# A copy of each scatter's row numbers on GpSimd, in an attention-and-experts block

## The chip, the cores and the metric

The kernel runs as one program on one core of a Trainium2 chip. The metric is the device time of one execution in microseconds (us), taken as the median of three runs. The engines named below are PE (TensorE, matrix products and transposes), DVE (VectorE), ACT (ScalarE), POOL (GpSimd) and SP (SyncE, which here only issues DMAs). Each engine takes its own instructions in the order in which they stand in the program.

## What is computed

The input `x` holds 4 sequences of 512 tokens with 128 features. A first half, a gated convolution block, replaces the attention. A second half is a mixture of 160 experts, of which each token takes 8. The heart of the second half, cut to what matters here (`x` is the normalized and modulated input of that half):

```python
probs = sigmoid(x @ router_w.T + expert_bias)
top_w, top_idx = top_k(probs, 8)
top_w = 2.5 * top_w / (sum(top_w) + 1e-9)
h1 = silu(einsum('th,eih->eti', x, w_gate))          # 160 experts, 64 inner columns
routed = einsum('eti,ehi->th', h1 * combine.T[:, :, None], w_down)   # combine: top_w at top_idx
out = routed + silu(x @ w_gate_shared.T) @ w_down_shared.T
x = x + gb * out
```

## The kernel before

The four sequences are handled one after the other by a generator, `sequence(b)`. Its pieces are interleaved by hand, so that the second half of one sequence runs beside the first half of the next. One sequence has 512 tokens, which lie on 128 partitions in 4 groups (`NT = 4`).

The experts don't compute every token. Each token is written 8 times into a table in device memory, once per chosen expert, at a row that belongs to that expert. There are two tables: `tables[0]` for sequences 0 and 1 and `tables[1]` for sequences 2 and 3, each with 17,408 rows of 128 numbers. Then `experts(s)` reads table `s` in 34 / 2 = 17 blocks of 1,024 rows (`xg`, a plain load issued by SP on L611), transposes each on PE (`px`, L616), multiplies by the experts' weights (`ph` on L639 and L675, `py` on L649 and L685), and stores the products in the same row order in `results[s]` (L629). Last, `combine(b)` fetches the 8 result rows of each token (`yk`, L725), weighs and adds them.

What happens around the change, in `sequence(b)`:

- DVE computes in `keys` (the 8 largest keys of a token), `ikey` (L491) and `slot_in` (L493) the table row of every token and choice: `slot_in` has 128 partitions, 4 groups and 8 choices, 32 row numbers per partition. The normalized tokens lie in `h2` (L433).
- Then come 4 x 8 = 32 scatters (L498). Each is one indirect DMA that POOL issues. It takes one column of `slot_in`, 128 row numbers, and writes 128 rows of 512 bytes from `h2[:, t, :]` to those rows of the table. The 32 scatters of a sequence are called a burst below. They are declared free of dependencies on each other. In four sequences there are 128 scatters.
- DVE later reads `slot_in` again (`row`, L544) to make the row numbers for the fetches.

POOL's other work: five small powers (L242) in the first 55 us, the 128 scatters, then in `combine` 128 indirect fetches (L725) and, for sequences 0 and 1 alone, a product of each fetched block with its weight (L702). In `combine` of those two sequences, the order fetch, product, fetch, product is written out by hand with `behind(b, "weight")` and `behind(b, "fetch")`. `behind(b, what)` lets instructions stand in their engine's order after the instruction that was noted in `last[what, b]`; it makes no wait.

`experts(0)` needs both bursts of table 0 to have landed, and is laid among the instructions of sequences 2 and 3. `experts(1)` needs the bursts of sequences 2 and 3. The fetches of sequences 0 and 1 need all of `results[0]`, and those of sequences 2 and 3 all of `results[1]`. POOL takes its instructions in order, so the fetches also come after all scatters.

Buffers: `own(b, shape, dtype, tag, name)` gives one buffer per tag and parity of `b`, so sequence `b + 2` takes over the buffers of sequence `b` and waits for their last readers. `keys` and, after the change, `pick` have the tag `"keys"`, so they share one buffer.

The order of instructions on each engine, where it isn't fixed by `behind`, is planned when the program is built, from estimated durations (`schedule_with_timeline_sim=True` in `kernel`). The planner also draws the semaphore waits. Adding instructions can thus shift the order of others.

Of the kernel before, what the change touches and what calls it, by code (L numbers as in the profile page):

```python
# [34 lines left out]
U32 = mybir.dt.uint32  # L35
# [5 lines left out]
P = 128  # L41
# [4 lines left out]
E, INTER, TOPK = 160, 64, 8  # L46
# [10 lines left out]
NT = L // P  # L57
# [35 lines left out]
def adaln_block(  # L93
    ctx: ExitStack, tc: tile.TileContext, x_rows, vecs, wmod, mats, lines, w_gd, w_dsT, w_ov, out_rows
):
    nc = tc.nc
# [19 lines left out]
    def own(b, shape, dtype, tag, name):  # L116
        return work.tile(shape, dtype, tag=f"{tag}{b % 2}", name=f"{name}_{b}", bufs=1)
# [24 lines left out]
    tables, results = [], []  # L142
    for i in range(2):
        t = dram.tile([ROWS, D], F32, tag=f"table{i}", name=f"table{i}")
        tables.append(t)
        t = dram.tile([ROWS, D], F32, tag=f"result{i}", name=f"result{i}")
# [32 lines left out]
    for eps in (1e-5, 1e-6):  # L179
# [7 lines left out]
        out=tri, in_=ones16, compare_op=ALU.is_gt, fill=0.0, base=0, pattern=[[1, P]], channel_multiplier=-1  # L187
# [88 lines left out]
    ready, halves, keep, last = {}, {}, {}, {}  # L276

    def behind(b, what):
        return tc.issue_after(last[what, b].ins) if (what, b) in last else nullcontext()
# [4 lines left out]
    def sequence(b):  # L284
# [61 lines left out]
        for k in range(DC):  # L346

            at, to, n = ds(32 * k, 32), max(0, 1 - k), L - abs(k - 1)
# [56 lines left out]
        for half in range(2):  # L405
            pl = bank(b, f"pl{b}_{half}")
            for i in range(2):
                t = 2 * half + i
# [13 lines left out]
        for half in range(2):  # L422
            for t in (2 * half, 2 * half + 1):
# [3 lines left out]
                    out=repl[:, t, :], in_to_replace=top[:, t, :], in_values=prob[:, t, :], imm_value=-1.0  # L427
                )
            at = ds(2 * half, 2)
# [33 lines left out]
        keys = own(b, [P, NT, TOPK], F32, "keys", "keys")  # L463
        k2 = ranks[:, 0:4, :].rearrange("p (h i) e -> p h i e", h=2)
        for half in range(2):
            pr = spare(ps_y, "y", f"pr{b}_{half}")
            for i in range(2):
                t = 2 * half + i
# [23 lines left out]
        slot_in = own(b, [P, NT, TOPK], U32, "slot_in", "slot_in")  # L492
        last["slots", b] = nc.vector.tensor_single_scalar(slot_in, ikey.bitcast(U32), 0x7FFF, ALU.bitwise_and)  # L493


        for t in range(NT):
            for k in range(TOPK):
                ins = nc.gpsimd.indirect_dma_start(  # L498
                    out=tables[b // 2], out_offset=bass.IndirectOffsetOnAxis(ap=slot_in[:, t, k : k + 1], axis=0),
                    in_=h2[:, t, :], in_offset=None, bounds_check=ROWS - 1, oob_is_err=False,  # L500
                ).ins
                tc.declare_no_dep(ins, group=f"dispatch{b // 2}", reason="different rows")
                tc.add_to_no_dep_group(f"dispatch{b // 2}", ins)

# [287 lines left out]


    parts = [sequence(b) for b in range(B)]
    w_pairs = [weights(g) for g in range(NGO - 2)]
    next(parts[0])
# [100 lines left out]
    with tc.If(flags[0] + flags[1] > 0):  # L897
# [7 lines left out]
        for part in range(3):  # L905
            for odd in range(2):
                at = sel4[:, :, odd, :, :]
                nc.gpsimd.affine_select(
                    out=at, in_=at, compare_op=ALU.not_equal, fill=1.0, base=-part * ECH - 3 * odd,
# [56 lines left out]
```

## Time and profile before

| What | Value |
|---|---|
| median of 3 runs | 467.53 us (467.45 to 467.7) |
| the profiled execution | 600.99 us |
| its span, first to last instruction | 599.3 us |
| POOL busy | 286.5 us of the span |
| DVE busy | 222.8 us |
| ACT busy | 149.7 us |
| scatters (L498) | 128, 128.6 us busy in all |
| fetches (L725) | 128, 125.0 us busy in all |

The profiled execution took 133 us longer than the median of the runs that weren't profiled. That gap is far larger than the difference between runs, so durations from the trace can't be added up to the median without asking which of them belong to both.

A row of the timeline gives the start and the duration in us, engine, line, operation, the written and the read tiles, the count, and in brackets the idle time before it with what ended it. A row of the table of waits gives the waiting engine, line and tile, then what it waited for, the total in us, the number of times and the longest. "Issue" means that the profile shows nothing that was waited for. "Remote", or "another core or an unknown queue", means that the wait's end has no event in the profile that could have ended it; on a program of one core it can't be another core.

The four bursts, from the timeline of POOL:

| Burst | first scatter starts | last scatter ends | length |
|---|---|---|---|
| sequence 0 | 71.29 | 113.83 | 42.5 us |
| sequence 1 | 136.73 | 178.30 | 41.6 us |
| sequence 2 | 212.86 | 254.35 | 41.5 us |
| sequence 3 | 292.39 | 333.19 | 40.8 us |

### The profile page before, as it was taken

What the parts mean: (1) busy time and instruction counts of PE and PEld (TensorE: products, weight loads), DVE (VectorE), ACT (ScalarE), POOL (GpSimd) and SP (SyncE); (2) the same over time, 40 slices, a digit from 0 to 9 for tenths busy, and PEclk for the clock granted to TensorE, in tenths of its full rate; (3) what the DMA queues carried; (4) which work ended last, traced back from release to release, by engine and by line L of the source; (5) the groups of instructions that cost most, each with busy time, mean ns of one, the idle gap of its engine ahead of it and who ended that gap; (6) DMA issues with size and microseconds to landing.
All of it is one profiled execution on the core that took longest, in us unless ns stands there. A gap on an engine that the chain in (4) does not pass through costs nothing.

```text
span 599.3 us, 7468 instructions
## 1 busy us (share of the span) xinstructions
PE 300.1 (50%) x2540; PEld 199.1 (33%) x2540; DVE 222.8 (37%) x747; ACT 149.7 (25%) x290; POOL 286.5 (48%) x334
## 2 busy tenths in 40 slices
PE   5998880399205973169721487847376640000000
PEld 3645440154102432147511365726265530000000
DVE  7637860288106490037700343201113202233332
ACT  2545331334105400044200121415155630000000
POOL 1001277406760067700377100088888707887773
PEclk9999795569755977568955587878599965555555
DMA  8999951003224021134841288956489941121211
GB/s 293 409 393 392 420 201 49 35 0 107 88 79 154 8 104 52 49 134 157 279 145 52 100 281 273 327 189 220 136 276 335 310 161 42 45 61 57 71 53 45
DMA packets 50366, 98.55 MB, mean 164 GB/s; under 512 B 7633, under 2 KB 26130, under 8 KB 48914
## 3 DMA queue, kind: packets, MB, share of 16 engines
q1 hardware_dynamic: 35856, 60.61, 28.9%
q10 hardware_dynamic: 6274, 20.62, 9.1%
q0 software_dynamic: 8192, 16.79, 8.9%
q8 instruction: 22, 0.36, 0.2%
q14 instruction: 22, 0.18, 0.1%
HBM read 50.54 MB, written 47.45 MB: 164 GB/s over the span
## 4 chain that ended last, share of the span: by engine, by line
PE 36%; another core or an unknown queue 20%; DMA 11%; issue 11%; POOL 10%; DVE 7%; ACT 3%; SPq 1%; ACTq 0%; DVEq 0%; POOLq 0%
POOL yk L725 9%; DMA xg<-table 7%; PE pc L356 5%; PE px L616 4%; PE py L649 3%; PE ph L321 3%; PE ph L675 3%; PE py L373 2%; PE ph L639 2%; DMA result<-yg 1%; PE pl L413 1%; DMA mat<-in_mats 1%; PE pu L345 1%; PE py L685 1%
## 5 line engine op out<-in xcount | busy, mean ns | idle before, releaser
L498 POOL DMA_INDIRECT table<-h,slot_in x128 | 128.6, 1005 | 151.5 <-DVE slot_in L493 60.9
L725 POOL DMA_INDIRECT yk<-result,row x128 | 125.0, 977 | 105.2 <-ACT yg L628 56.2
L616 PE MATMUL px<-ident,xg 128*128 128x128 f32 x272 | 49.8, 318 | 28.5 <-DMA xg<-table 16.9
L649 PE MATMUL py<-w_g,h 64*64 64x128 f32 x640 | 31.5, 329 | 50.8 <-ACT h L644 28.0
L616 PEld LDWEIGHTS px<-ident,xg 128*128 128x128 f32 x272 | 34.8, 160 | 39.4 <-issue 29.7
L649 PEld LDWEIGHTS py<-w_g,h 64*64 64x64 f32 x640 | 23.9, 163 | 57.2 <-ACT h L644 30.2
L709 DVE SCALAR_TENSOR_TENSOR out_sb<-yk,wk,out_sb 128x128 f32<-128x128 f32 x56 | 20.0, 356 | 52.3 <-DMA yk<-result,row 52.1
L639 PE MATMUL ph<-xs,w_g 128*64 128x64 f32 x640 | 32.8, 247 | 8.0 <-issue 7.3
L627 ACT COPY yg<-py 128x512 f32<-128x512 f32 x34 | 19.9, 585 | 67.7 <-PE py L649 41.0
L711 DVE TENSOR_TENSOR out_sb<-out_sb,yk 128x128 f32<-128x128 f32 x48 | 14.8, 314 | 57.6 <-POOL yk L702 43.6
L617 DVE COPY xs<-px 128x512 f32<-128x512 f32 x34 | 22.6, 684 | 35.7 <-remote 19.5
L356 PE MATMUL pc<-val,dia 128*128 128x512 f32 x72 | 32.0, 595 | 0.0
L639 PEld LDWEIGHTS ph<-xs,w_g 128*64 128x64 f32 x640 | 26.8, 155 | 13.9 <-issue 11.1
L386 DVE TENSOR_TENSOR x<-po,h 128x512 f32<-128x512 f32 x4 | 2.8, 692 | 76.7 <-remote 76.1
L303 PE MATMUL px_h<-ident,hn 128*128 128x128 f32 x16 | 3.9, 374 | 54.2 <-ACT hn L302 32.1
L644 ACT ACTIVATE h<-ph 128x512 f32<-128x512 f32 x20 | 11.9, 597 | 66.8 <-remote 57.7
L702 POOL TENSOR_TENSOR yk<-yk,wk 128x128 f32<-128x128 f32 x64 | 26.1, 414 | 1.0
L361 DVE SCALAR_TENSOR_TENSOR s<-val,vec,s 128x512 f32<-128x512 f32 x32 | 24.0, 750 | 0.7
L685 PE MATMUL py<-ow,h 64*128 64x128 f32 x224 | 16.8, 291 | 11.4 <-ACT h L680 8.4
L321 PE MATMUL ph<-hf,in_wn 128*128 128x512 f32 x32 | 20.6, 785 | 1.7 <-ACT hf L305 1.7
L617 ACT COPY xs<-px 128x512 f32<-128x512 f32 x34 | 18.9, 589 | 9.8 <-PE px L616 5.7
L303 PEld LDWEIGHTS px_h<-ident,hn 128*128 128x128 f32 x16 | 2.5, 161 | 55.9 <-ACT hn L302 32.7
(230 smaller groups left out, 528.7 us busy)
## 6 DMA issues: line engine op xcount, KB each, us to landing
table<-early SPq DMA_DIRECT2D x2, 8704.0 KB
xg<-table SPq DMA_DIRECT2D x34, 512.0 KB
result<-yg ACTq DMA_DIRECT2D x34, 512.0 KB
ow<-in_w_ov SPq DMA_DIRECT2D x112, 96.0 KB
w_g<-in_w_gd SPq DMA_DIRECT2D x10, 1024.0 KB
table<-h,slot_in POOLq DMA_INDIRECT x128
yk<-result,row POOLq DMA_INDIRECT x128
prob_kept<-prob ACTq DMA_DIRECT2D x4, 320.0 KB
```

Source lines behind the costliest of these rows:

```text
L321: nc.tensor.matmul(ph, in_wn[:, ts(o, P)], hf, start=True, stop=True)
L356: nc.tensor.matmul(pc, dia[:, k, :], val[:, 0, k : k + L], start=(k == 0), stop=(k == KS - 1))
L361: last["conv", b] = nc.vector.scalar_tensor_tensor(s[:, 1, :], val[:, 1, k : k + L], v("sym_k", KS + k), s[:, 1, :], ALU.mult, ALU.add)
L498: ins = nc.gpsimd.indirect_dma_start(out=tables[b // 2], out_offset=bass.IndirectOffsetOnAxis(ap=slot_in[:, t, k : k + 1], axis=0), in_=h2 ...
L616: nc.tensor.transpose(px[:, c, :], xg[:, 4 * half + c, :], ident)
L617: (nc.scalar.copy if s else nc.vector.tensor_copy)(xs[:, ds(4 * half, 4), :], px)
L639: nc.tensor.matmul(ph[ds((r ^ (j & 1)) * INTER, INTER), j, :], w[:, j, 0, ds(r * INTER, INTER)], xs[:, :, ds(16 * j + 8 * r, 8)], start=Tr ...
L649: nc.tensor.matmul(py[j & 1][ds(r * BLK, BLK), j // 2, :], h[at, j, :], w[at, j, 1, :], start=True, stop=True)
L685: nc.tensor.matmul(py[r][:, c, :], h[at, c, :], ow[at, c, r, ds(r * INTER, D)], start=True, stop=True)
L702: last["weight", b] = nc.gpsimd.tensor_mul(row, row, wk[:, t, k : k + 1].to_broadcast([P, D]))
L709: nc.vector.scalar_tensor_tensor(acc, yk[:, k, :], wk[:, t, k : k + 1], acc, ALU.mult, ALU.add)
L725: last["fetch", b] = nc.gpsimd.indirect_dma_start(out=yk[:, k, :], out_offset=None, in_=results[b // 2], in_offset=bass.IndirectOffsetOnAx ...
```

## The change

Each scatter no longer takes its row numbers from `slot_in`. POOL first copies the 128x1 column to a tile `pick` of the same shape (32-bit unsigned), and the scatter takes them from there. `behind(b, "scatter")` puts each copy after the scatter before it in POOL's order. Since the scatter reads what the copy wrote, it waits for that copy. The bounds check, the rows written and the table are the same.

```diff
+        pick = own(b, [P, NT, TOPK], U32, "keys", "pick")
         for t in range(NT):
             for k in range(TOPK):
-                ins = nc.gpsimd.indirect_dma_start(
-                    out=tables[b // 2], out_offset=bass.IndirectOffsetOnAxis(ap=slot_in[:, t, k : k + 1], axis=0),
+
+                at = pick[:, t, k : k + 1]
+                with behind(b, "scatter"):
+                    last["pick", b] = nc.gpsimd.tensor_copy(at, slot_in[:, t, k : k + 1])
+                last["scatter", b] = nc.gpsimd.indirect_dma_start(
+                    out=tables[b // 2], out_offset=bass.IndirectOffsetOnAxis(ap=at, axis=0),
                     in_=h2[:, t, :], in_offset=None, bounds_check=ROWS - 1, oob_is_err=False,
-                ).ins
+                )
+                ins = last["scatter", b].ins
                 tc.declare_no_dep(ins, group=f"dispatch{b // 2}", reason="different rows")
                 tc.add_to_no_dep_group(f"dispatch{b // 2}", ins)
```

## The prediction

> **What bounds the kernel now.** I read the chain of waits in order of time first, then the table of waits, then POOL's timeline, then PE's where the experts begin. The chain's longest pieces:
>
> ```profile
> 91.30 17.72 another core or an unknown queue
> 114.38 3.26 another core or an unknown queue
> 156.69 25.70 another core or an unknown queue
> 225.75 32.65 another core or an unknown queue
> 299.27 22.83 another core or an unknown queue
> 322.71 14.83 another core or an unknown queue
> ```
>
> Each row is a start, a length and what held the chain. All six lie inside a burst of scatters or just behind it, and end at the latest 4.4 us after the burst does (258.40 against 254.35, 337.54 against 333.19). Together they are 117.0 us. The table of waits names who stood there:
>
> ```profile
> DVE x L386 <- remote: 76.1, 3, 32.6
> ACT h L644 <- remote: 57.7, 4, 25.3
> POOL table L498 <- DVE slot_in L493: 60.9, 2, 38.0
> POOL yk L725 <- DMA result<-yg: 18.7, 1, 18.7
> ```
>
> DVE and ACT wait for nothing that the profile can show, L386 takes only `po` and `h`, and PE had done `po` by then. POOL meanwhile goes on at an even pace. So the other engines stand still while POOL scatters, for no reason of data.
>
> Do the unprofiled runs have this standstill? Take the 117.0 us out. The fetches, which start at 389.43, would start at 272.4. The POOL chain from there is 87.6 us of fetches and products (389.43 to 477.0), then the 18.7 us wait for the last results, then 103.5 us (495.76 to 599.3). PE has two unexplained waits of 6.24 and 6.56 us at 399 and 427 in that part, and in 389 to 440 does 340 matmuls against 553 in the 50 us after; without that the 18.7 us wait should nearly vanish. 272.4 + 87.6 + 103.5 is 463.5, plus 1.7 around the span (600.99 - 599.3) is 465.2. The median is 467.5. So I read the standstill as belonging to the profiled execution alone, and all but 2.3 us of the timed runs as explained without it. In them the bound is: the sequences and `experts(0)`, up to 272, then POOL with its fetches to the end.
>
> POOL's pace, first in a burst, then in a fetch with a product between:
>
> ```profile
> 174.78 0.97 POOL L498 DMA_INDIRECT table<-h,slot_in  x1 [0.30 <-issue]
> 176.06 0.97 POOL L498 DMA_INDIRECT table<-h,slot_in  x1 [0.30 <-issue]
> ...
> 508.98 0.41 POOL L702 TENSOR_TENSOR yk<-yk,wk 128x128 f32<-128x128 f32 x1
> 509.55 1.02 POOL L725 DMA_INDIRECT yk<-result,row  x1 [0.16 <-issue]
> 510.58 0.42 POOL L702 TENSOR_TENSOR yk<-yk,wk 128x128 f32<-128x128 f32 x1
> 511.16 1.02 POOL L725 DMA_INDIRECT yk<-result,row  x1 [0.16 <-issue]
> ...
> 587.12 0.94 POOL L725 DMA_INDIRECT yk<-result,row  x1 [0.30 <-issue]
> 588.37 0.94 POOL L725 DMA_INDIRECT yk<-result,row  x1 [0.30 <-issue]
> ```
>
> From start to start a scatter takes 1.275 us, a bare fetch 1.25, a fetch with a product 1.61. The product adds 0.36, though it lasts 0.41: it fills part of the 0.30 us that lies empty between two bare DMAs.
>
> **What the Trainium skill says.** Perfetto Trace Analysis, section "GPSIMD Engine Instruction": a GpSimd span in a profile is unreliable, and one should go by start-to-start spacing. The rows agree (0.97 shown, 1.275 paced), so I price by spacing. The same page, "DMA Instruction — SWDGE (GPSIMD)": the shown end is that of descriptor generation, not of the data. The trace agrees: the last fetch ends at 590.55, and DVE uses it at 592.25, 1.7 us later. GPSIMD Engine Reference, section "2.1 Instruction dispatch": every Pool instruction is broadcast and dispatched by software, some tens of cycles, so a 128x1 copy is nearly all overhead. The 128x1 IOTA at 1.27 us with 0.13 fits. SBUF — State Buffer, section "Who interferes with whom": a DVE instruction with two SBUF inputs contends with a GpSimd instruction that reads SBUF. The copies read SBUF; no row of this trace shows the effect.
>
> **The change, part by part.** Removed: nothing but the scatter's direct reading of `slot_in`. Added: 128 copies on POOL, and in each scatter a wait for its copy. Moved: nothing by hand; the planned order can shift.
>
> *A copy.* No row shows a 128x1 copy on POOL. The 128x1 memsets at the start last 0.10, the IOTA 0.13, the 128x128 product 0.41. I take 0.13.
>
> *The wait.* No row shows POOL waiting for its own result. A scatter that waited for `slot_in` in burst 3 started 0.28 us after it (292.11 to 292.39); in bursts 1 and 2, 0.27 and 0.28. That is my figure. Lower end: 0.16, the gap after a product. Upper end: 0.45, if the wait makes POOL's sequencer hold the scatter back undecoded; the first scatters of bursts 0 to 2 last 1.57, 1.59 and 1.38 in place of 0.97, so a cold start can cost that much and more.
>
> *The cycle.* Scatter 0.97, plus 0.04 as fetches after a product are longer by that at least (0.98 to 1.02 against 0.94), 0.03 to the copy, copy 0.13, wait 0.28: 1.45 us, 0.175 more than now. Lower end: 0.97 + 0.03 + 0.10 + 0.16 = 1.26, a little under today's 1.275. Upper end: 1.02 + 0.03 + 0.25 + 0.45 = 1.75; the middle of the upper part, 1.6, I price below.
>
> *Where it lies.* In time without standstill, `slot_in` is ready for the four bursts at 71.3, 115.75 (136.73 less 21.0), 166.2 (212.86 less 46.7) and 213.1 (292.39 less 79.3), and a burst lasts 40.8 to 42.5. POOL idles 2 to 9 us between bursts. With 32 x 0.175 = 5.6 us more, burst 0 ends at 119.4, burst 1 starts then and ends at 166.6 (157.3 before), burst 2 at 213.7, burst 3 at 260.2. The fetches start at 272.4, so POOL's own queue keeps 12 us of slack. Behind a waiting scatter stand only the next copies and scatters of POOL.
>
> *Who waits for the burst.* `experts(0)`. Its first load needs bursts 0 and 1 landed (1.7 us) and takes about 4.0 (the chain has an `xg` load of 4.04): ready at 163.0 before, 172.3 after. PE reaches it here:
>
> ```profile
> 215.70 1.11 PE L616 MATMUL px<-ident,xg 128*128 128x128 f32 x4 [1.64 <-DVE key L516]
> 217.75 1.11 PE L616 MATMUL px<-ident,xg 128*128 128x128 f32 x4 [0.94 <-DVE xs L617]
> 219.07 5.22 PE L373 MATMUL py<-s,w_sym 128*128 128x512 f32 x8 [0.20 <-ACT s L364]
> ```
>
> 215.70 less 46.7 is 169.0. There were 6.0 us of cover; after, the load is 3.3 us late. PE is in order, and behind these transposes stands L373 of sequence 3, on the chain. So up to 3.3 us reach the path. Some is absorbed: PE idles 1.64 and 0.94 us there anyway, and a planner that sees longer bursts would put the transposes later. I take 2.0 us. Burst 3 and `experts(1)` have 12 us of cover; the fetches and everything after 272 are untouched.
>
> *DVE against the copies.* At most 32 x 0.13 = 4.2 us per burst if every copy met a two-input DVE instruction; DVE is busy 14.1 of 20 us at the start of burst 0, and only a part of that with such instructions. I take one us, beside PE's work: nothing on the path. The shared `keys` buffer makes sequence b + 2 wait for burst b, over long before: nothing.
>
> Sum: 467.5 + 2.0 = 469.5 us, made on the standstill-free account of the profiled execution and laid onto the median.
>
> **Rivals.**
> A, the forecast: a cycle of about 1.45, 469.5 us (467.8 to 472).
> B, hidden: the cycle stays under 1.37, as the copy fills the empty 0.30 us; burst 1 ends within the 6.0 us of cover; 467.5. For it: the product costs less than it lasts. Against it: the product waits for no copy.
> C, POOL becomes the bound: a cycle of 1.6. Burst 1 ends at 71.3 + 84.1 + 64 x 0.325 = 176.2, the load is ready at 181.9, 12.9 us late: 480.4. The fetches would be 6.9 us late, inside that. From 1.545 on, POOL's queue alone reaches 272.4.
> D, the other side: the timed runs do have some of the standstill, and a Pool instruction between two scatters relieves it, as PE stands less in the fetches with products. It decides as soon as the relief exceeds A's 2 us. With my account only 2.3 us are left unexplained, which gives 465.2 with copies hidden. If fetches in timed runs are faster than in the profile, the unexplained part and the gain are larger, 10 us or more. A luckier planned order falls here too, by a few us.
> That the copies do not stand between the scatters is excluded, as the scatter reads the copy.
>
> **How the numbers follow.** A measurement of this kernel tells a change from none at about 0.2%, 0.93 us. Chances: A 0.42 (0.36 beyond 468.5, 0.06 inside), B 0.18 (0.16 inside, 0.02 under), C 0.13, D 0.27, of which 0.08 under 462. So faster 0.29, same 0.22, slower 0.49. The range from 462 to 480 leaves out the far part of D and half of C. The likeliest case alone: 467.8 to 472.
>
> **What would show it.** Copies of about 0.13 us in POOL's timeline, scatters 1.4 to 1.5 us apart, bursts of 45 to 48 us. In the profiled execution the standstill may shrink a great deal, so its span may fall by tens of us while the median hardly moves; that would confirm the account above. A median that falls by more than 1% would refute it: then the standstill is in the timed runs too. Scatters 1.6 us apart or more mean C.

## The result, and the profile after

| | kernel before | kernel after |
|---|---|---|
| median | 467.49 us (4 runs, 464.45 to 467.7) | 482.46 us (4 runs, 481.26 to 483.67) |
| profiled execution | 600.99 us, span 599.3 | 481.98 us, span 480.3 |

The change makes the kernel 3.4% slower: the ratio is 1.0336, with an interval of 1.03 to 1.0371. That is 15 us where 2 were forecast, and just above the range of 462 to 480. The profiled execution of after takes as long as its unprofiled runs. Lines below L498 stand six lines further down in the new kernel: the copy is L502, the scatter L503, the transposes of the experts L622, the fetches L731, the products L708.

The page of after, engines first, then the costliest groups (busy us, mean ns of one, idle time before them and what ended most of it):

```profile
PE 276.9 (58%) x2540; PEld 185.6 (39%) x2540; DVE 223.9 (47%) x747; ACT 149.4 (31%) x290; POOL 321.0 (67%) x462
...
L503 POOL DMA_INDIRECT table<-h,pick x128 | 132.7, 1037 | 37.9 <-POOL pick L502 35.9
...
L622 PE MATMUL px<-ident,xg 128*128 128x128 f32 x272 | 46.3, 311 | 52.1 <-DMA xg<-table 49.5
...
L502 POOL COPY pick<-slot_in 128x1 uint32<-128x1 uint32 x128 | 30.1, 235 | 22.8 <-DVE slot_in L493 22.2
```

POOL has 34.5 us more work (321.0 against 286.5): the copies' 30.1 and 4.1 more in the scatters. Beside that stand 35.9 us in which scatters wait for their copies. None of it says yet what reaches the end. For that, look at the third group: the experts' transposes wait 49.5 us for the loads of their blocks. PE's timeline shows where:

```profile
158.06 1.16 PE L589 MATMUL psh<-wds,hs 64*128 64x128 f32 x8 [0.68 <-ACT hs L586]
179.57 1.09 PE L622 MATMUL px<-ident,xg 128*128 128x128 f32 x4 [20.36 <-DMA xg<-table]
181.45 1.12 PE L622 MATMUL px<-ident,xg 128*128 128x128 f32 x4 [0.78 <-DVE xs L623]
182.77 3.78 PE L373 MATMUL py<-s,w_sym 128*128 128x512 f32 x4 [0.20 <-ACT s L364]
```

A single wait of 20.36 us, and L373 of sequence 3, which has nothing to do with that block, stands behind it. POOL's timeline gives the pace. First beside DVE, at the head of burst 0; then undisturbed, at the end of burst 1; last the first fetch:

```profile
72.70 0.68 POOL L502 COPY pick<-slot_in 128x1 uint32<-128x1 uint32 x1
73.66 1.43 POOL L503 DMA_INDIRECT table<-h,pick  x1 [0.28 <-POOL pick L502]
75.10 0.75 POOL L502 COPY pick<-slot_in 128x1 uint32<-128x1 uint32 x1
...
172.41 0.98 POOL L503 DMA_INDIRECT table<-h,pick  x1 [0.28 <-POOL pick L502]
173.40 0.19 POOL L502 COPY pick<-slot_in 128x1 uint32<-128x1 uint32 x1
173.87 0.98 POOL L503 DMA_INDIRECT table<-h,pick  x1 [0.28 <-POOL pick L502]
...
289.86 1.00 POOL L731 DMA_INDIRECT yk<-result,row  x1 [13.57 <-DMA xg<-table]
```

The undisturbed cycle is 0.98 + 0.19 + 0.28 = 1.45 us, as predicted. The disturbed one is 2.46 (a scatter of 1.43, a copy of 0.75, the wait of 0.28). DVE's timeline at that moment:

```profile
72.59 0.75 DVE L361 SCALAR_TENSOR_TENSOR s<-val,vec,s 128x512 f32<-128x512 f32 x1
73.26 0.32 DVE L522 TENSOR_TENSOR key<-key,pn 128x160 f32<-128x160 f32 x1
73.49 2.33 DVE L361 SCALAR_TENSOR_TENSOR s<-val,vec,s 128x512 f32<-128x512 f32 x3
75.74 0.17 DVE L550 TENSOR_SCALAR row<-slot_in 128x32 uint32<-128x32 uint32 x1
```

Both long copies end just after an instruction of L361 does (73.38 beside 73.34, 75.85 beside 75.82). L361 reads two tiles of 512 columns and a column of scalars (`vec`) from SBUF. The section "Who interferes with whom" of the Trainium skill's page SBUF — State Buffer says that a DVE instruction with two SBUF inputs contends with a GpSimd instruction that reads SBUF, and that their shared ports are an exclusive lock. The trace agrees in the main: these copies take 0.68 and 0.75 us where an undisturbed one takes 0.19, and all 15 copies of the trace that last over 0.3 us end 0.02 to 0.06 us after a DVE instruction does; of the other 113, 18 do. But not every overlap costs: copies at 70.58 and 115.54, which started just after an instruction of L361, took 0.18 and 0.19.

### The profile page after: what moved, and what is told of

Its sections match the earlier page's. It is cut to its first block, busy times and chain, and to the rows that moved or that the text cites. A ratio compares the mean times of both kernels' runs of the same rounds, so it can differ in the third digit from the quotient of the medians.

```text
span 480.3 us, 7716 instructions
## 1 busy us (share of the span) xinstructions
PE 276.9 (58%) x2540; PEld 185.6 (39%) x2540; DVE 223.9 (47%) x747; ACT 149.4 (31%) x290; POOL 321.0 (67%) x462
## 5 line engine op out<-in xcount | busy, mean ns | idle before, releaser
L503 POOL DMA_INDIRECT table<-h,pick x128 | 132.7, 1037 | 37.9 <-POOL pick L502 35.9
L731 POOL DMA_INDIRECT yk<-result,row x128 | 125.3, 979 | 44.0 <-issue 28.8
L622 PE MATMUL px<-ident,xg 128*128 128x128 f32 x272 | 46.3, 311 | 52.1 <-DMA xg<-table 49.5
L622 PEld LDWEIGHTS px<-ident,xg 128*128 128x128 f32 x272 | 33.9, 158 | 60.5 <-issue 42.9
L502 POOL COPY pick<-slot_in 128x1 uint32<-128x1 uint32 x128 | 30.1, 235 | 22.8 <-DVE slot_in L493 22.2
L645 PE MATMUL ph<-xs,w_g 128*64 128x64 f32 x640 | 27.8, 240 | 0.0
L655 PE MATMUL py<-w_g,h 64*64 64x128 f32 x640 | 24.7, 297 | 4.6 <-ACT h L650 4.5
L708 POOL TENSOR_TENSOR yk<-yk,wk 128x128 f32<-128x128 f32 x64 | 26.2, 414 | 1.1
L645 PEld LDWEIGHTS ph<-xs,w_g 128*64 128x64 f32 x640 | 23.9, 150 | 4.7 <-issue 2.6
L361 DVE SCALAR_TENSOR_TENSOR s<-val,vec,s 128x512 f32<-128x512 f32 x32 | 24.0, 751 | 0.7
L655 PEld LDWEIGHTS py<-w_g,h 64*64 64x64 f32 x640 | 19.2, 144 | 8.6 <-ACT h L650 5.9
L356 PEld LDWEIGHTS pc<-val,dia 128*128 128x128 f32 x72 | 13.4, 189 | 16.7 <-issue 16.7
L691 PEld LDWEIGHTS py<-ow,h 64*128 64x128 f32 x224 | 13.6, 187 | 13.3 <-ACT h L686 12.8
```

The source lines that it names most:

```text
L356: nc.tensor.matmul(pc, dia[:, k, :], val[:, 0, k : k + L], start=(k == 0), stop=(k == KS - 1))
L361: last["conv", b] = nc.vector.scalar_tensor_tensor(s[:, 1, :], val[:, 1, k : k + L], v("sym_k", KS + k), s[:, 1, :], ALU.mult, ALU.add)
L502: last["pick", b] = nc.gpsimd.tensor_copy(at, slot_in[:, t, k : k + 1])
L503: last["scatter", b] = nc.gpsimd.indirect_dma_start(out=tables[b // 2], out_offset=bass.IndirectOffsetOnAxis(ap=at, axis=0), in_=h2[:, t, ...
L622: nc.tensor.transpose(px[:, c, :], xg[:, 4 * half + c, :], ident)
L645: nc.tensor.matmul(ph[ds((r ^ (j & 1)) * INTER, INTER), j, :], w[:, j, 0, ds(r * INTER, INTER)], xs[:, :, ds(16 * j + 8 * r, 8)], start=Tr ...
```

## The experiments

The theory after the result: the loss comes through one place. Burst 1 ends late, the first load of `experts(0)` is late by as much, and PE, which takes its instructions in order, passes on the whole delay to sequence 3. The rival: the loss comes from all bursts, or from POOL's own queue up to the fetches.

### Copies in one pair of sequences alone

```diff
-        pick = own(b, [P, NT, TOPK], U32, "keys", "pick")
+        pick = own(b, [P, NT, TOPK], U32, "keys", "pick") if b < 2 else None
...
+                at = pick[:, t, k : k + 1] if b < 2 else slot_in[:, t, k : k + 1]
+                if b < 2:
```

The second run has `b >= 2` in the same three places.

> Copies in bursts 0 and 1 alone. Theory 'late first block': the whole loss comes from the end of burst 1, which holds back the first load of table 0 and with it PE; so the time stays at 481 to 484 us, and PE waits some 20 us for its first xg, as in the changed kernel. Rival 'POOL's queue': the loss is the sum of all slower bursts, so half of the copies cost about half, 474 to 476. In the profiled execution the standstill of the other engines should be gone in bursts 0 and 1 and stay in 2 and 3, if a Pool instruction between two scatters is what ends it.

> Copies in bursts 2 and 3 alone. Theory 'late first block': no loss, 466.5 to 469 us, since bursts 2 and 3 have time until experts(1). Rival 'POOL's queue': about half of the loss, 474 to 476. In the profiled execution the standstill stays in bursts 0 and 1 and goes in 2 and 3.

Measured: with copies in sequences 0 and 1, 483.62 us, ratio 1.04 (1.0234 to 1.0566), the whole loss. With copies in sequences 2 and 3, 467.8 us, ratio 1.0042 (1.0003 to 1.0082). In the first, PE waited 19.60 us for its first block, in the second 6.37. Neither profile has a standstill, in any burst, so what both expectations say of it stayed untested here.

### The copy without the wait, and an instruction without a read

```diff
-                at = pick[:, t, k : k + 1]
+                at = slot_in[:, t, k : k + 1]
                 with behind(b, "scatter"):
-                    last["pick", b] = nc.gpsimd.tensor_copy(at, slot_in[:, t, k : k + 1])
+                    last["pick", b] = nc.gpsimd.tensor_copy(pick[:, t, k : k + 1], at)
```

In the other run that last line is `nc.gpsimd.memset(pick[:, t, k : k + 1], 0)`. In both, the scatters read `slot_in`.

> The copy stands between the scatters as in the change, but the scatter takes its rows from slot_in, so it doesn't wait for the copy. If the wait of 0.28 us is a price of its own, the clean cycle falls from 1.45 to about 1.36 us (0.98 + 0.03 + 0.19 + 0.16), burst 1 ends 6 us earlier or more, and the time is 474 to 477 us. If the copy's own time and its collisions with DVE are the price, the cycle stays at 1.45 and the time at 480 or more.

> A memset of the same 128x1 column stands in place of the copy, so nothing between the scatters reads memory, and no scatter waits for it. If DVE's instructions with two SBUF inputs hold up the copies, the spread of the cycle goes with the reading: mean close to the median, about 1.3, and a time of 468 to 472 us. If the collisions cost nothing, it equals the run without the wait.

Measured: 473.19 us, ratio 1.0162 (1.0046 to 1.0279), without the wait; 466.61 us, ratio 0.9994 (0.9956 to 1.0033), with the memset. POOL's timeline in burst 1, without the wait, then with the memset:

```profile
150.97 0.98 POOL L503 DMA_INDIRECT table<-h,slot_in  x1 [0.16 <-issue]
151.95 0.19 POOL L502 COPY pick<-slot_in 128x1 uint32<-128x1 uint32 x1
152.30 0.98 POOL L503 DMA_INDIRECT table<-h,slot_in  x1 [0.16 <-issue]
```

```profile
150.89 0.97 POOL L503 DMA_INDIRECT table<-h,slot_in  x1 [0.19 <-issue]
151.85 0.12 POOL L502 MEMSET pick<- 128x1 uint32 x1
152.16 0.97 POOL L503 DMA_INDIRECT table<-h,slot_in  x1 [0.19 <-issue]
```

From scatter to scatter: 1.33 and 1.27 us, against 1.45 with the wait and 1.28 in the kernel before. So of the 0.17 us that a cycle costs when undisturbed, the wait is 0.12 (0.28 in place of 0.16), the copy 0.05. In the time of the kernel, some 9 of the 15 us go with the wait, the rest with the copy. A memset of 0.12 to 0.13 us vanishes in the gap of 0.30 us that lies between two bare scatters anyway: 0.19 + 0.12 = 0.31. It is hardly stretched beside DVE: its mean is 135 ns, the copy's 235, and eight memsets that lie wholly inside an instruction of L361 take 0.11 to 0.14 us. Both times lie a little under what was expected. The memset's bursts are also no more even than those of the kernel before (burst 0: mean spacing 1.41 us, median 1.28): beside DVE some scatters last longer by themselves, with or without copies.

### The kernel before once more, one large copy, and PE's order

> The kernel before, unchanged, profiled once more: its recorded execution of 600.6 us held 117.0 us of standstill in which no engine worked. Theory 'the standstill belonged to that one execution': span near 465.5 us, no gap of microseconds in which all engines rest, burst 1 ends near 157 us, and the first transposes of the experts' phase start at 161 to 163 us after 4 to 7 us of waiting for their load, so that there was no cover at all before the change. Rival 'recording this kernel brings it': span again near 600 us with pieces of tens of us. Rival 'the cover of 6.0 us was there': the same transposes wait for nothing and start near 169 us.

Measured: 464.15 us, span 462.4, and no row of "another core or an unknown queue" in the chain. PE's timeline of this execution of the kernel before, and POOL's first fetch:

```profile
156.14 1.16 PE L583 MATMUL psh<-wds,hs 64*128 64x128 f32 x8 [0.68 <-ACT hs L580]
162.62 1.09 PE L616 MATMUL px<-ident,xg 128*128 128x128 f32 x4 [5.32 <-DMA xg<-table]
164.49 1.11 PE L616 MATMUL px<-ident,xg 128*128 128x128 f32 x4 [0.79 <-DVE xs L617]
165.81 1.22 PE L373 MATMUL py<-s,w_sym 128*128 128x512 f32 x1 [0.20 <-ACT s L364]
```

```profile
271.88 0.99 POOL L725 DMA_INDIRECT yk<-result,row  x1 [20.12 <-DMA ow<-in_w_ov]
```

There was no cover. PE stood at this block from 157.3 on and waited 5.32 us, already before the change (6.37 and 5.31 us in the versions with copies in the last pair and with the memset, whose first two bursts are as fast). After the change the first transposes start 16.95 us later (179.57 less 162.62) and the first fetch 17.98 us later (289.86 less 271.88); the two profiled executions differ by 17.83 us. From the first fetch to the end of the last, it is 183.0 us here (271.88 to 454.92) and 182.9 after (289.86 to 472.78). So nothing is won or lost after that fetch.

Next, all row numbers in one copy ahead of the burst, 128x32, and the scatters read `pick`:

```diff
+        pick = own(b, [P, NT, TOPK], U32, "keys", "pick")
+        nc.gpsimd.tensor_copy(pick, slot_in)
...
+                at = pick[:, t, k : k + 1]
```

> One GpSimd copy of all 128x32 row numbers ahead of each burst, the scatters read the second tile. Theory 'the price is 128 small instructions with their waits': one copy of 0.2 to 0.5 us a burst, median spacing of scatters back at 1.28 us, burst 1 ends at 157 to 159 us, time 466 to 469 us (the kernel before). Rival 'reading the row numbers from the second tile costs': spacing stays at 1.40 us or more and the time is 475 us or more.

Measured: 467.37 us, ratio 1.0014 (0.9988 to 1.0039), scatters 1.28 us apart. Its groups, kept apart by shape:

```profile
L502 POOL DMA_INDIRECT table<-h,pick x128 | 131.8, 1030 | 39.5 <-issue 37.8 <-POOL pick L497 1.7
...
L497 POOL COPY pick<-slot_in 128x32 uint32<-128x32 uint32 x4 | 1.0, 239 | 28.4 <-DVE slot_in L493 28.4
```

A copy of 32 columns takes 239 ns, hardly more than a copy of one. Reading from a second tile costs nothing. Nor do 128 small instructions as such, as the memsets show; what costs is 128 copies between the scatters, with their reads and with the waits for them.

Then PE's order. In the changed kernel the first block's transposes go behind sequence 3's last logits matmul; in the kernel before, behind its output matmuls:

```diff
-                for c in range(4):
-                    nc.tensor.transpose(px[:, c, :], xg[:, 4 * half + c, :], ident)
+                with behind(B - 1, "logits1") if s == 0 and g == 0 else nullcontext():
+                    for c in range(4):
+                        nc.tensor.transpose(px[:, c, :], xg[:, 4 * half + c, :], ident)
```

> The changed kernel with its copies, the transposes of the first block of experts placed behind sequence 3's last logits matmul in TensorE's order. Theory 'the loss is the in-order wait of TensorE for the first block's load': bursts as slow as in the changed kernel at first (burst 1 ends at 173 to 176 us), but TensorE goes on with sequence 3's stages and most of the loss comes back: 467 to 474 us. Rival 'the later scatters themselves set the end, whatever TensorE does': time stays at 478 to 484 us.

> The kernel before, the transposes of the first block of experts placed behind sequence 3's output matmuls. Theory 'before the change TensorE already waited some 5 us for this load': burst 1 ends near 157 us as before, the wait of 4 to 7 us goes, time 462 to 467 us. Rival 'the load was covered before the change, so there is nothing to win': 467 to 470 us, or more where the moved block holds up the experts' phase.

Measured: the changed kernel with it 477.71 us, ratio 1.0247 (1.0171 to 1.0324); the kernel before with it 462.42 us, ratio 0.9907 (0.9881 to 0.9934). The second is as the theory has it. The first is not: 4 to 5 us come back, not 8 to 15. The new wait, in PE's timeline of the changed kernel with the late block:

```profile
263.17 1.09 PE L682 MATMUL ph<-xs,ow 128*64 128x128 f32 x16
274.80 1.94 PE L623 MATMUL px<-ident,xg 128*128 128x128 f32 x8 [10.53 <-DMA xg<-table]
276.67 2.08 PE L692 MATMUL py<-ow,h 64*128 64x128 f32 x16
```

and SP's queue at the same moment (the second `xg` load of the first row leaves at the row's end):

```profile
255.54 16.12 SPq L617 DMA_DIRECT2D xg<-table  x2
272.50 1.91 SPq L672 DMA_DIRECT2D ow<-in_w_ov  x4
```

Burst 3 ends at 270.01 there, and the load released then is the first of `experts(1)`. The last products of `experts(0)` (L692 at 276.67), which the fetches need, stand behind its transposes on PE. The first fetch starts at 284.63, 5.2 us earlier than in the changed kernel, and the end follows 182.7 us later. So the loss has two doors of the same kind, one for each table; closing one opens the other.

### The first fetch as the measure

For the kernels with the first block in its old place, each from its profiled execution, all on chips of the first kind (see below):

| kernel | burst 1 ends | first fetch starts | time |
|---|---|---|---|
| before, once more | 157.57 | 271.88 | 464.15 |
| copies in sequences 2 and 3 | 157.06 | 275.12 | 467.20 |
| one large copy | 157.70 | 274.43 | 466.55 |
| memset | 159.82 | 275.31 | 467.28 |
| copy without wait | 164.98 | 279.43 | 471.21 |
| copies in sequences 0 and 1 | 174.14 | 288.08 | 480.80 |
| after | 174.85 | 289.86 | 481.98 |

From the first row to the last it is 17.83 us of time for 17.28 us of burst, and in every row the time is 191.8 to 192.7 us more than the start of the first fetch. Single executions of one kernel spread over some 6 us (464.2 to 471.0 for the second row), so the small steps between rows mean nothing. For the same reason the 17.8 us between two single executions stand beside 15 us between the medians: 2.6 us of them come from burst 0 starting later (71.47 against 68.90), and kernels without copies in it start it anywhere from 68.9 to 71.6.

### Products off POOL, and a surprise

The chain from the first fetch on is POOL's own. To take 64 products from it, VectorE weighs the rows of all sequences within its additions:

```diff
-            if b < 2:
-                last["weight", b] = nc.gpsimd.tensor_mul(row, row, wk[:, t, k : k + 1].to_broadcast([P, D]))
+            pass
...
-            if b >= 2 and k == 0:
+            if k == 0:
...
-            elif b >= 2:
+            else:
...
-                if b >= 2 or len(pending) > 5:
+                if True:
```

The three kernels are the one before, the one before with the late block, and the changed one with the late block.

> The kernel before, without copies: the 64 weighing products of sequences 0 and 1 leave GpSimd and are made on VectorE inside its additions, as for sequences 2 and 3. Theory 'from the end of experts(0) on, GpSimd's own queue of fetches and products sets the end': fetches stand 1.25 to 1.30 us apart throughout, 64 x 0.36 us = 23 us less for GpSimd, time 443 to 452 us. Rival 'the second half of the experts sets it': gain of at most 5 us, 462 us or more.

> The kernel before with the products on VectorE and the first block of experts placed behind sequence 3's output matmuls. Theory 'the two gains lie on different stretches': 3 to 5 us less than the kernel that has the products moved alone, 438 to 448 us. Rival 'one hides the other': within 1 us of it.

> The changed kernel with its copies, the first block placed behind sequence 3's last logits matmul, and the products on VectorE. Theory 'what is left of the loss is TensorE waiting for bursts 2 and 3 at the head of experts(1)': that wait of 8 to 12 us stays, the end of TensorE's work some 10 to 14 us behind that of the version without copies, time 448 to 458 us, 8 to 15 us above it. Rival 'what is left is GpSimd's backlog alone': with GpSimd relieved, within 4 us of the version without copies.

Measured: 644.42, 642.21 and 574.6 us. But the kernel before, on the same chip, took 599.75 us (7 runs, 596.33 to 601.38), where in all runs up to then, apart from the first profile, it had taken 462 to 471. All three expectations failed, and for a reason that none of them held: on this chip every run, profiled or not, takes as long as the first profile, and the profiles taken on it show the same standstill. So it isn't a property of one execution, and not of profiling. And there the version with copies (and with the products moved and the block late) is the fast one, 0.9569 (0.9512 to 0.9626) of the kernel before, while the version with the products moved is slower, 1.0782 (1.0705 to 1.0858). The table of waits of the products' kernel:

```profile
POOL yk L722 <- issue: 115.9, 123, 78.7
PEld py L649 <- issue: 86.8, 29, 41.7
ACT h L644 <- remote: 83.8, 3, 43.7
DVE x L386 <- remote: 74.3, 3, 32.9
```

POOL's wait of 78.7 us is for the results of `experts(1)`: it had run 64 bare fetches, from 388.6 to 468.6, and while it did so, the other engines stood still (ACT for 43.7 us from 393.5 on, the weight loads of PE for 41.7), so that these results were missing afterwards. In the kernel before, a product stands between most of these fetches, and in its first profile ACT's longest waits of this sort beside them are 8.8 and 8.9 us.

### Both kinds of chips

> The changed kernel, unchanged, on the chip that this call gets, beside the kernel before on the same chip. Theory 'two kinds of chips': where the kernel before takes 463 to 471 us, this one takes 480 to 485; where the kernel before takes 595 to 602 us, this one takes 480 to 520 us, since an instruction between two scatters lets the other engines work. Rival 'the change costs the same 15 us everywhere': 610 to 617 us on a chip of the second kind.

> The version that took 642.21 us where the kernel before took 599.75 us: the products on VectorE, the first block of experts placed behind sequence 3's output matmuls, no copies. Theory 'GpSimd's queue sets the end where there is no standstill': 438 to 448 us beside 467 us; on a chip with the standstill again 630 to 650 us, as its fetches have no instruction between them. Rival 'the moved products themselves slow the kernel down': slower than before on either kind of chip.

> A memset of one column on GpSimd between any two scatters, which read slot_in as before, and the first block placed behind sequence 3's output matmuls; fetches as in the kernel before. Theory 'any instruction between two indirect DMAs is enough and a memset lies in their gap': 459 to 466 us on a chip without standstill; on a chip with it 465 to 510 us, below the changed kernel. Rival 'only the wait on the copy breaks the standstill': 580 us or more on such a chip.

> As the one with memsets between scatters and the late first block, and a memset after each fetch of sequences 2 and 3 too, where no product stands between. Theory 'a memset costs nothing in the gap of two indirect DMAs': within 2 us of the version without memsets between fetches on a chip without standstill; on a chip with it equal or up to 20 us less. Rival 'memsets cost 0.13 us each there': 4 to 8 us more.

> The changed kernel beside the kernel before, on whatever chip this call gets. Theory 'two kinds of chips': 480 to 485 us where the kernel before takes 463 to 471 us; 480 to 520 us where the kernel before takes 595 to 602 us. Rival 'the same price everywhere': 610 to 617 us on a chip of the second kind.

> The changed kernel beside the kernel before, on whatever chip this call gets. Theory 'two kinds of chips': 478 to 485 us where the kernel before takes 463 to 471 us; 480 to 520 us where the kernel before takes 595 to 602 us. Rival 'the same price everywhere': 610 to 617 us on a chip of the second kind.

> The products on VectorE, the first block of experts placed late, and a memset of one column on GpSimd between any two scatters and any two fetches. On a chip without standstill: 443 to 450 us, as the version without memsets (446.58 us), if a memset lies in the gap of two indirect DMAs in the fetches too; 450 to 460 us if each costs its 0.13 us. On a chip with the standstill: 445 to 490 us if any instruction between two indirect DMAs is enough; 600 us or more if only the wait on a copy is.

The memset versions put `nc.gpsimd.memset(pick[:, t, k : k + 1], 0)` behind each scatter, and for the fetches (`pad` is one more tile of the shape of `pick`)

```diff
+                    with behind(b, "fetch"):
+                        last["weight", b] = nc.gpsimd.memset(pad[:, t, k : k + 1], 0)
```

Measured, by the time that the kernel before takes on the same chip; three chips were of the first kind, two of the second:

| kernel | where before takes 462 to 471 | where before takes 591 to 604 |
|---|---|---|
| changed | 480.71, 481.64 | 530.56 (2 runs, 525.96 to 535.15) |
| late block (before) | 462.42 | not run |
| late block, memsets between scatters | 461.75 | not run |
| the same, and between fetches of 2 and 3 | 463.9 | not run |
| products on DVE | not run | 644.42 |
| late block, products on DVE | 446.58 | 642.21 |
| the same, memsets everywhere | not run | 649.11 (641.66 to 653.89) |
| changed, late block, products on DVE | not run | 574.6 |

The ratios of the changed kernel on the first kind are 1.0274 (1.0205 to 1.0343) and 1.028 (1.0181 to 1.0379). On the second it stood beside 597.52 us (7 runs, 591.32 to 603.95): 67 us faster, and the runs of the two don't overlap, though it missed the 480 to 520 us that were expected. Between the two versions with the products moved and the block late, copies make as much: 574.6 against 642.21. The long pieces in its chain of waits there, in order of time:

```profile
185.69 5.75 another core or an unknown queue
194.31 4.48 another core or an unknown queue
202.84 1.84 another core or an unknown queue
247.81 12.05 another core or an unknown queue
272.03 1.82 another core or an unknown queue
374.89 1.39 another core or an unknown queue
```

They sum to 27.3 us where the kernel before had 117.0; nothing is left of the standstill in bursts 0 and 1, which end at 171.07, and most of what is left lies beside bursts 2 and 3, although these have copies too. The memsets do nothing of the kind: with one between any two indirect DMAs, the kernel took 649.11 us, ratio 1.0871 (1.0721 to 1.102), where the same kernel without memsets took 642.21 on the other chip of this kind.

The versions that beat both kernels on the first kind are the late block (462.42) and, above all, the late block with the products on DVE: 446.58 us, ratio 0.9537 (0.9466 to 0.9609). On the second kind that last one takes 642.21 us beside 599.75, 7% more.

What the two kinds of chips differ in isn't known. Each chip of the second kind was seen in one stretch of runs only, so a passing state of the chip isn't ruled out, and it isn't on record on which chip the first profile was taken. The kernel before was also granted a lower mean clock there (0.72 to 0.74 against 0.78 to 0.81). But the profile page of after shows half clock in the last nine of its 40 slices, where PE rests, so the lower mean may follow from the standstill rather than cause it.

What shortens the standstill stays open, too. A copy whose scatter waits for it does (a cycle of 1.45 us), and the products between fetches seem to; a memset, which writes alone and leaves the cycle at 1.28, doesn't. Whether it is the read, the wait or the longer cycle wasn't separated: the copy without the wait was run on the first kind of chip only.

## Why the prediction was wrong

1. **The standstill.** Half right. The timed runs of the first kind are explained without it: the kernel before, profiled again, takes 464.15 us, and 465.2 had been worked out. "Belonging to the profiled execution alone" was wrong: on two chips every run shows it. The sign that the prediction named, a profiled span that falls by tens of us, did come (599.3 to 480.3), but by luck: the unchanged kernel, profiled again, fell to 462.4 as well. Rival D's mechanism, an instruction between two scatters that relieves the standstill, exists in part: copies do, worth 67 us on a chip of the second kind, memsets don't. But it isn't in the runs that were compared.

2. **"There were 6.0 us of cover", the step that failed.** The time without standstill was made by taking off the rows of the chain, 46.7 us up to there. These rows don't hold all of the standstill. Set beside the second profile of the same kernel, DVE's row for burst 2's row numbers shows the true offset. The first execution, then the second:

```profile
212.40 0.18 DVE L493 TENSOR_SCALAR slot_in<-ikey 128x32 uint32<-128x32 uint32 x1
```

```profile
155.64 0.35 DVE L493 TENSOR_SCALAR slot_in<-ikey 128x32 uint32<-128x32 uint32 x1
```

212.40 less 155.64 is 56.8 us, ten more than 46.7. PE's arrival at 169.0 should have read 158.9. POOL's end of burst 1 had come out right (worked out as 157.3, measured 157.57), partly by luck, as the bursts really begin earlier and last longer. So the two sides of one comparison were on different clocks, and 6.0 us of cover were in truth 5.3 us of waiting. With that alone, the whole shift of 9.3 us would have counted, not 2.0: some 477 us.

The same error had put 1.9 us of idle time on POOL between bursts 0 and 1, which took up part of burst 0's growth. In the second profile burst 1's row numbers are there nearly 5 us before POOL comes to them, and the bursts follow each other without a break:

```profile
109.54 0.20 DVE L493 TENSOR_SCALAR slot_in<-ikey 128x32 uint32<-128x32 uint32 x1
```

```profile
112.97 1.24 POOL L498 DMA_INDIRECT table<-h,slot_in  x1 [0.30 <-issue]
114.52 1.27 POOL L498 DMA_INDIRECT table<-h,slot_in  x1 [0.30 <-DVE s L361]
```

3. **The cycle, and the bursts.** The clean cycle of 1.45 us was exact by luck: the copy takes 0.19 us in place of 0.13, while the scatter takes 0.98 in place of 1.01, and the 0.03 up to the copy doesn't show (172.41 + 0.98 is 173.39, and the copy starts at 173.40). The mean wasn't: 1.684 in burst 0 and 1.572 in burst 1, 1.479 and 1.541 in the others. Burst 1 ends at 174.85, not 166.6. Against the second profile of before, burst 0 grew by 7.9 us (45.31 to 53.19) and burst 1 by 6.7 (43.05 to 49.71), where 5.6 each were taken. "DVE against the copies ... nothing on the path" was the mis-sized term: bursts 0 and 1 lie beside much of DVE's work, and they are on the path. In burst 0, 31 copies take 9.30 us where 0.19 each would be 5.9; in burst 1, 32 take 7.69 where it would be 6.1. So the copies were stretched by 3.4 and 1.6 us there, not by one us at no cost. The first profile hid part of DVE's effect on bursts, probably because DVE stood still during them: bare bursts 0 last 41.7 to 42.5 us in all profiles with a standstill, and 44.9 to 45.8 in all without.

   Together: 7.9 and 6.7 us more in the two bursts, with no cover, no idle time between them and nothing absorbed, on 467.5 make 482.1 us. The median is 482.46.

4. **Rival C** came close to the time with 480.4, and with bursts nearly as they came (burst 1 at 176.2 against 174.85), through the late load. In part that is luck: its bursts grow by 20.8 us together, more than the 14.5 measured, and the cover that it too counted on takes off what was too much. And its name was wrong: POOL didn't become the bound. It idles 13.57 us before the first fetch, so POOL's slack, estimated at 12 us, held.

5. **The fetches and what follows** are untouched, as said: 183.0 and 182.9 us.

## What to carry to other kernels

A stretch of profile in which engines stand still must be taken out of every engine's clock by matching rows, best against a second profile; a chain of waits gives only part of it, and a cover of a few us made that way is worth nothing. When an in-order engine meets a late load early in its program, what counts is everything behind it; placing that block later gave 4 to 5 us in both kernels here, and in the changed one no more than that, since the next load of its kind then did the same. Between indirect DMAs on GpSimd, one copy for a whole burst (239 ns for 32 columns) is free where 32 small ones with their waits cost 5 to 8 us; and a change like this should be judged on more than one chip.

## What the runs showed of the hardware that wasn't expected

- Two kinds of chips: the same kernel takes 462 to 471 us on three of them and 591 to 604 on two. On the latter, PE, ACT and DVE stand still for up to 44 us while GpSimd runs bare indirect DMAs, scatters 1.28 us apart and fetches 1.25 us apart alike.
- A GpSimd memset of one column (0.12 to 0.13 us) fits into the gap between two indirect DMAs at no cost, for scatters (1.27 us apart) and fetches. The fetches with memsets, in POOL's timeline of the version that has them for sequences 2 and 3, are 1.25 us apart, as bare ones are. From the first fetch to the end of the last it is 182.7 us there and 183.3 without them, so the 2 us between the two medians (463.9 and 461.75) don't come from the fetches:

```profile
419.07 0.94 POOL L733 DMA_INDIRECT yk<-result,row  x1 [0.19 <-issue]
420.00 0.12 POOL L739 MEMSET pad<- 128x1 uint32 x1
420.32 0.94 POOL L733 DMA_INDIRECT yk<-result,row  x1 [0.19 <-issue]
```

- A scatter that waits for the GpSimd copy just ahead of it starts 0.28 us after that copy's end; without the wait, 0.16.
